# Stage ranks, delta-A weights on GpSimd and a last pair kept in SBUF, in a scan, attention and FFN kernel on one core

## The chip, the cores and the metric

The kernel runs on one core of a Trainium2 chip. The metric is the device time of one execution in microseconds. Engines are named as in the profile: PE (matmul), PEld (its weight loads), DVE (VectorE), ACT (ScalarE), POOL (GpSimd), and SP, whose queue issues all of this kernel's DMAs.

## What is computed

The input is x of shape (8, 96, 64, 64). Layer 0 is a selective-scan block with a residual, layer 1 an attention without softmax and a feed-forward with values rounded to 8-bit floats, each with a residual. Cut to what matters here:

```python
xh = layernorm(gn(x))                       # group norm, then layer norm over 96 channels
xi, z = split(xh @ in_proj.T)               # 192 channels each
xi = silu(depthwise_conv3x3(xi))            # 64 x 64 image
xs = [rows, columns, rows reversed, columns reversed](xi)      # K = 4 orders
dts, B, C = split(x_proj[k] @ xs[k])
delta = softplus(dt_proj[k] @ dts)
h = exp(delta * A) * h + (delta * u) * B;  y = sum(h * C)       # scan over 4096 steps
out = out_proj(layernorm(sum of 4 orders) * silu(z));  x = x + out
t = t + attention(ln(t));  t = t + ffn(ln(t))                   # per token of 96 channels
```

A is a weight, -exp(A_log). Eight images are worked on as four pairs.

## The kernel before

For each pair the function `vss_attn_ffn` runs three stages, and work of the pair before shares the first two:

1. **Project** (`project`, L369) with `back` (L825) of the previous pair. `project` normalises the two images in 16 blocks of 512 pixels and multiplies by the input weights; xi goes to padded tiles `ybuf` in SBUF and silu(z) to DRAM (`zs`). `back` adds the four scan orders in 16 blocks, transposes on PE (L880), normalises, projects out, adds the residual (`ta`, the new x) and normalises it for the attention (`tns`). It stores `ta` and `tns` to DRAM (`t1`, `tn`) and sums the attention's key-value products on PE (`pm`). When all 16 blocks are in, it makes one 97x96 matrix per image, `hm`.
2. **Convolve and prepare** (`convolve` L457, `prepare` L503) with `tail` (L963) of the previous pair. `convolve` does channel tiles 0 and 2 on DVE (L473 and L476: for each half of the image nine instructions of 2048 elements for each tile) and tile 1 on PE (nine matmuls with diagonal matrices per block of 512), then silu on ACT. `prepare` goes over two orders (rows, columns) of 8 chunks; in a chunk, for two directions and three tiles, it makes what the notes here call a unit: softplus on ACT (`d`), du = d*u on DVE (L560), and d split in three bf16 parts (ACT, DVE `rest` L571, ACT, POOL `dp` L576), stored to DRAM as `du` and `dl`. That is 96 units. The column order first copies xi transposed to `u` on POOL (L535). `tail` loads `t1` and `tn` again in 16 blocks and does the attention's matmul with `hm`, a norm and the feed-forward.
3. **Scan** (`scan`): 1024 scan instructions on DVE (L743) for each pair, with 512 products on POOL (L707).

After the fourth pair's scan, `back` of that pair runs alone, and then `tail` of it alone.

**What sets the order.** Stages 1 and 2 record their operations in a `Plan`, with an engine, a cost, what they read and write, the ring of buffers that they take, and a rank. `Plan.run` then writes the program: again and again it takes the operation that can start first by these costs, and among those of an engine that could start within 0.1 us of its earliest, the one of lowest rank. An engine executes its instructions in the order written. The ranks in stage 2 are -2 for the convolution's first half of the image and -1 for its second (`-2 + h`), -1 + c/10 for the silus of chunk c, 0 to 1 for prepare's chunks ((o * NCH + c) / 16), and i/16 for the tail's blocks. Rings hold back blocks: `P.ring("chunk", [None] * 3)` lets three blocks of project be under way, and the PSUM banks of 2 KB are named rings, `q=3, hold=2`. In `norm` (L355) a `hold` bank is taken by the first matmul (L357) and given back by the last multiply (L365); between lie a square, a matmul (L361), ln and exp.

**The weights of delta * A** are made once, between stages 1 and 2 of the first pair, by `decay_weights` (L282), outside any `Plan`. DVE negates exp(A_log), splits it in three bf16 parts (L291 to L296), which are stored to DRAM (`ad`) and read back in another layout (`ac`, L311); for each of four directions DVE multiplies 128 x 6144 elements by a mask (L317) and SP stores the product (`awd`, L322). The product's operands are a broadcast of `ac` along its third axis and of the mask along its second and fourth:

```python
nc.vector.tensor_tensor(aw,                                   # [128, 48, 16, 8] bf16
    ac.rearrange("p (c n) -> p c n", n=8).unsqueeze(2).to_broadcast([128, 48, 16, 8]),
    mask.unsqueeze(1).unsqueeze(3).to_broadcast([128, 48, 16, 8]), ALU.mult)
```

The pool of these tiles is closed before `xi`'s is opened (`xp`, after `decay_weights()`).

Of the kernel before, what the change touches and what calls it, by code (L numbers as in the profile page):

```python
# [10 lines left out]
F32 = mybir.dt.float32  # L11
# [145 lines left out]
def vss_attn_ffn(ctx: ExitStack, tc: tile.TileContext, a: dict):  # L157
# [124 lines left out]
    def decay_weights():  # L282
# [4 lines left out]
        with tc.tile_pool(name="aprep", bufs=1) as wp:  # L287
            am = wp.tile([128, KD, 2, NS], F32, name="am")
            nc.sync.dma_start(am, a["alog"])
            nc.scalar.activation(am, am, AF.Exp)  # L290
            nc.vector.tensor_scalar(am, am, -1.0, None, ALU.mult)  # L291
            for i in range(3):
                ap = wp.tile([128, KD, 2, NS], BF16, name=f"ap{i}")
                nc.vector.tensor_copy(ap, am)
                if i < 2:
                    nc.vector.tensor_tensor(am, am, ap, ALU.subtract)  # L296
                for k in range(KD):
                    nc.sync.dma_start(ad[i, k, 0:128], ap[:, k, 0])
                    nc.sync.dma_start(ad[i, k, 128:DI], ap[0:64, k, 1])
# [8 lines left out]
            for k in range(KD):  # L308
                ac = wp.tile([128, NE * NS], BF16, name="ac", bufs=2)
                for i, rows, n in ((0, slice(0, 96, 2), 6), (1, slice(1, 96, 2), 6), (2, slice(96, 128), 4)):  # L310
                    nc.sync.dma_start(  # L311
                        ac[rows],
                        ad[i, k].rearrange("(s c) n -> s (c n)", s=8).unsqueeze(0)
                        .to_broadcast([n, 8, NE * NS]),
                    )
                aw = wp.tile([128, 48, 16, 8], BF16, name="awp", bufs=2)
                nc.vector.tensor_tensor(  # L317
                    aw,
                    ac.rearrange("p (c n) -> p c n", n=8).unsqueeze(2).to_broadcast([128, 48, 16, 8]),
                    mask.unsqueeze(1).unsqueeze(3).to_broadcast([128, 48, 16, 8]), ALU.mult,  # L320
                )
                nc.sync.dma_start(awd[k], aw.rearrange("p c m n -> p (c m n)"))  # L322
# [45 lines left out]

    def project(P, pair, zs, ybuf, p1):  # L369

# [10 lines left out]
        ring(P, p1, "zt", 2, [128, 2, F])  # L381
        P.ring("chunk", [None] * 3)
        stat = [[p1.tile([DIM, w], F32, name=f"{n}{b}") for n, w in (
# [73 lines left out]
    def convolve(P, xi, ybuf, p1):  # L457
# [3 lines left out]
        for t in range(9):  # L461
            dve(P, 0.28, lambda t=t: nc.vector.tensor_scalar(
                diag[:, t, :], ident, convw[:, 0, t : t + 1], None, ALU.mult), (), (f"diag#{t}",), (), -2)
        for h in range(2):
            for T in (0, 2):
                for t in range(9):
# [5 lines left out]
                    if t == 0:  # L472
                        dve(P, 1.4, lambda o=o, v=v, w=w: nc.vector.tensor_scalar(  # L473
                            o, v, w, None, ALU.mult), (), wr, (), -2 + h)
                    else:
                        dve(P, 2.34, lambda o=o, v=v, w=w: nc.vector.scalar_tensor_tensor(  # L476
                            o, v, w, o, ALU.mult, ALU.add), (), wr, (), -2 + h)
            for c in range(4 * h, 4 * h + 4):
                r0 = c * ROWS
                n = f"pc.{c}"  # L480
                for t in range(9):
                    dy, dx = divmod(t, 3)
                    mm(P, 0.87, lambda n=n, t=t, r0=r0, dy=dy, dx=dx: nc.tensor.matmul(  # L483
                        P[n], diag[:, t, :], pad[1][:, r0 + dy : r0 + dy + ROWS, dx : dx + HH],
                        start=(t == 0), stop=(t == 8)), (f"diag#{t}",), (n,), ((n, "big"),), -2 + h)
                act(P, lambda c=c: xi[1][:, bass.ts(c, F)], lambda n=n: P[n], AF.Identity, 0.68, (n,),
                    (f"xi1#{c}",), (), -2 + h, bias=convb[:, 0:1])
        for c in range(NCH):
            for T in range(3):
                b_ = 0.0 if T == 1 else convb[:, half(T) : half(T) + 1]  # L490
                act(P, lambda T=T, c=c: xi[T][:, bass.ts(c, F)], lambda T=T, c=c: xi[T][:, bass.ts(c, F)],
                    AF.Silu, 0.72, (), (f"xi{T}#{c}",), (), -1 + c / 10, "silu", bias=b_)

# [330 lines left out]

    def back(P, pair, ys, us, zs, t1, tn, tmp, psm):  # L825
        tns = ring(P, tmp, "tns", 3, [DIM + 1, F])
        for i, t in enumerate(tns):
            nc.gpsimd.memset(t[DIM : DIM + 1], 1.0)
        ring(P, tmp, "yk", 2, [128, KD, 8, 4 * NE])
# [5 lines left out]
        ring(P, tmp, "g", 2, [DIM, 2, F])  # L835
        ring(P, tmp, "ta", 2, [DIM, F])
        ring(P, tmp, "kv", 2, [128, 2, 2, DIM])
# [3 lines left out]
        for i in range(2 * NCH):  # L841
# [120 lines left out]

    def tail(P, pair, t1, tn, tmp):  # L963
        tfs = ring(P, tmp, "tf", 3, [DIM + 1, F])
        for t in tfs:
            nc.gpsimd.memset(t[DIM : DIM + 1], 1.0)
        ring(P, tmp, "xa", 3, [DIM, F])
        ring(P, tmp, "t2", 4, [DIM, F])
# [4 lines left out]
        ring(P, tmp, "ot", 2, [DIM, F])  # L973
        P.ring("unit", [None] * 3)
        for i in range(2 * NCH):
            c, b = divmod(i, 2)
            cs = bass.ts(c, F)
            rank = i / 16
            n = f"t.{i}"
            tf, xa, pa, t2, tq, hq, p2, y16, ot = (  # L980
                v + n for v in ("tf", "xa", "pa", "t2", "tq", "hq", "p2", "y16", "ot"))
            dma(P, 0.2, lambda tf=tf: P[tf][0:DIM], lambda b=b, cs=cs: tn[b, :, cs], (), (tf,), ((tf, "tf"),), rank)
            dma(P, 0.2, lambda xa=xa: P[xa], lambda b=b, cs=cs: t1[b, :, cs], (), (xa,), ((xa, "xa"),), rank)
            P.unit = f"unit.{n}"
            mm(P, 0.9, lambda pa=pa, b=b, tf=tf: nc.tensor.matmul(  # L985
                P[pa][:DIM], hm[b], P[tf], start=True, stop=True), (tf,), (pa,), ((pa, "q"),), rank)
            dve(P, 0.69, lambda t2=t2, xa=xa, pa=pa: nc.vector.tensor_tensor(
# [36 lines left out]
    for pair in range(npair + 1):  # L1024
# [11 lines left out]
        with ExitStack() as pads, ExitStack() as xis:  # L1036
# [4 lines left out]
            with ExitStack() as st:  # L1041
                st.enter_context(tc.manual_schedule())
                P = Plan()
                tmp = st.enter_context(tc.tile_pool(name="bk", bufs=1))
                psum = banks(P, st, q=3, hold=2, **({"py": 2} if old else {}))
                ring(P, tmp, "small", 6 if old else 8, [DIM, F])
                if old:
                    back(P, pair - 1, old["ys"], old["us"], old["zs"], old["t1"], old["tn"], tmp, psum)
                if new:
                    project(P, pair, new["zs"], ybuf,  # L1050
                            st.enter_context(tc.tile_pool(name="p1", bufs=1, side="right")))
                P.run(table)
# [5 lines left out]
            with ExitStack() as st:  # L1058
# [128 lines left out]
```

## Time and profile before

| what | us |
|---|---|
| median of 3 runs | 10556.45 |
| lowest and highest | 10539.96 and 10565.98 |
| the profiled execution, and its span | 10552.56 and 10550.8 |
| first scan instruction of pairs 0 to 3, from the span's start | 638.9, 3228.7, 5821.8, 8417.2 |
| end of the last scan instruction of pairs 0 to 3 | 2414.6, 5005.4, 7598.9, 10192.6 |
| first instruction of the convolution on DVE, pairs 0 to 3 | 230.5, 2729.4, 5320.1, 7914.2 |
| last dp on POOL, pairs 0 to 3 | 614.6, 3204.3, 5796.7, 8390.8 |
| last pair: hm made; last block of the tail; end of the span | 10437.7; 10547.3; 10550.8 |

Times in the profile run from the span's start. A group's line gives line, engine, operation, the tiles written and read, and a count; behind the bar come busy time, the mean of one in ns, and the idle time before them with who ended it. In a table by stretch each engine has its busy us and its count of instructions. The clock column is the share of TensorE's clock that was granted, the DMA column the mean busy share of the 16 DMA engines.

### The profile page before, as it was taken

Reading aid. Unit: us, or ns where it says so; the run is one execution under the profiler, and the core shown is the slowest. Engines: PE = TensorE matmul, PEld = TensorE weight load, DVE = VectorE, ACT = ScalarE, POOL = GpSimd, SP = SyncE. Lnnn points to the kernel's source line nnn. Section 1 sums busy time; section 2 is a strip of 40 time slices with the busy share of each in tenths; the row PEclk is TensorE's granted clock in tenths of the full one; section 3 lists DMA queues with packets and bytes.
Section 4 is the critical chain, followed back from the end, with each engine's and each line's share of the span. In section 5 each row is a group of like instructions: output and inputs, shape, how many; then the busy total and the mean of one; then the engine's idle time right before and its main releaser. Section 6 shows DMA issues by size and latency. Waiting matters only on the chain. (4 is left out here: it accounts for less than half of the span.)

```text
span 10550.8 us, 377529 instructions
## 1 busy us (share of the span) xinstructions
PE 7647.5 (72%) x163328; PEld 5376.1 (51%) x163328; DVE 9068.0 (86%) x6702; ACT 6962.8 (66%) x12201; POOL 7996.9 (76%) x2802
## 2 busy tenths in 40 slices
PE   6766666668985676666987666776698666666678
PEld 2235555555324565555532555665553255555554
DVE  3689999996668999999566999999857699999985
ACT  3567777775566777776656677777665577777754
POOL 0579999992148999999124999999812599999961
PEclk8679999999878989999987889889897799989999
DMA  2787888879478888787947888888775778787885
GB/s 75 203 212 212 217 214 214 217 212 203 123 192 213 214 214 216 211 218 192 210 131 194 213 214 215 214 214 215 195 181 159 192 213 216 213 215 215 214 200 138
DMA packets 1597751, 2095.56 MB, mean 199 GB/s; under 512 B 407603, under 2 KB 1048116, under 8 KB 1592500
## 3 DMA queue, kind: packets, MB, share of 16 engines
q1 hardware_dynamic: 1596084, 2071.39, 75.6%
q8 instruction: 1283, 21.02, 0.9%
q14 instruction: 384, 3.15, 0.1%
HBM read 1606.82 MB, written 464.01 MB: 196 GB/s over the span
## 5 line engine op out<-in xcount | busy, mean ns | idle before, releaser
L743 DVE TENSOR_TENSOR_SCAN h<-da,dbu 128x774 f32<-128x774 f32 x4096 | 7026.7, 1759 | 128.2 <-POOL dbu L707 43.4
L707 POOL TENSOR_TENSOR dbu<-dut,bc 128x1536 f32<-128x1536 f32 x2048 | 7083.5, 3601 | 60.8 <-DMA dm<-dl 42.4
L732 ACT ACTIVATE da<-da 128x768 f32<-128x768 f32 x4092 | 3260.2, 797 | 1985.0 <-PE da L725 1970.1
L725 PE MATMUL da<-dm,aw 128*128 128x128 bf16 x24576 | 2282.4, 235 | 2329.8 <-DVE h L743 2089.6
L725 PEld LDWEIGHTS <-aw 128*128 128x128 bf16 x24576 | 1793.6, 104 | 2574.9 <-issue 2287.7
L761 PE MATMUL yp<-h,cw 128*32 128x48 f32 x131072 | 2902.4, 238 | 78.7 <-issue 65.7
L761 PEld LDWEIGHTS yp<-h,cw 128*32 128x32 f32 x131072 | 2410.2, 154 | 527.2 <-issue 207.0
L661 ACT ACTIVATE cw<-bc,blk 128x512 f32<-128x512 f32 x2048 | 1472.6, 720 | 81.5 <-DMA dm<-dl 81.5
L576 POOL TENSOR_TENSOR dp<-rest,dp 128x512 bf16<-128x512 f32 x384 | 456.8, 1194 | 665.3 <-ACT dp L332 620.0
L866 POOL TENSOR_TENSOR yd<-yk 128x768 f32<-128x768 f32 x64 | 125.6, 1962 | 779.6 <-DMA yk<-ys 407.1
L535 POOL COPY u<-xi 128x512 f32<-128x512 f32 x96 | 205.3, 2153 | 534.4 <-ACT xi L332 502.1
L555 PE MATMUL big<-S,dtw 12*128 12x512 f32 x768 | 521.1, 805 | 120.2 <-ACT d L332 96.0
L769 ACT ACTIVATE yev<-yp 128x384 f32<-128x384 f32 x1024 | 505.6, 494 | 64.5 <-PE yp L761 64.2
L571 DVE TENSOR_TENSOR rest<-d,dp 128x512 f32<-128x512 f32 x384 | 345.0, 904 | 207.6 <-ACT dp L332 161.2
L332 ACT ACTIVATE dp<-rest 128x512 bf16<-128x512 f32 x384 | 239.2, 628 | 304.6 <-DVE rest L571 303.5
L704 ACT COPY dbu<-h 128x12 f32<-128x12 f32 x1984 | 409.3, 206 | 0.0
L555 PEld LDWEIGHTS big<-S,dtw 12*128 12x128 f32 x768 | 157.7, 231 | 439.0 <-ACT d L332 225.7
L332 ACT ACTIVATE small<-hold 96x512 f32<-96x512 f32 x192 | 113.8, 593 | 313.5 <-PE hold L357 295.8
L560 DVE TENSOR_TENSOR du<-d,u 128x512 f32<-128x512 f32 x192 | 210.1, 1102 | 118.9 <-ACT d L332 118.9
L880 PEld LDWEIGHTS py<-ident,yd 128*96 128x96 f32 x2048 | 245.4, 165 | 91.2 <-issue 83.9
L476 DVE SCALAR_TENSOR_TENSOR xi<-y,c_convw,xi 128x2048 f32<-128x2048 f32 x128 | 290.3, 2347 | 0.0
L483 PE MATMUL big<-y,diag 128*128 128x512 f32 x576 | 260.2, 615 | 18.3 <-ACT xi L332 12.5
(122 smaller groups left out, 6009.5 us busy)
## 6 DMA issues: line engine op xcount, KB each, us to landing
dut<-du SPq DMA_DIRECT2D x2048, 384.0 KB
dm<-dl SPq DMA_DIRECT2D x1024, 288.0 KB
dl<-dp SPq DMA_DIRECT2D x256, 384.0 KB
dm<-dl SPq DMA_DIRECT2D x1024, 96.0 KB
ys<-yev SPq DMA_DIRECT2D x1024, 96.0 KB
du<-du SPq DMA_DIRECT2D x256, 256.0 KB
bc<-cs SPq DMA_DIRECT2D x512, 128.0 KB
bc<-bs SPq DMA_DIRECT2D x512, 128.0 KB
```

Source lines behind the costliest of these rows:

```text
L332: "ACT", cost, lambda: nc.scalar.activation(dst(), src_(), func, **kw),
L555: mm(P, 1.0, lambda pq=pq, k=k, T=T, S=S: nc.tensor.matmul(P[pq], dtw[64:76, k, T], P[S][64:76], start=True, stop=True), (S, "dtw"), (pq,) ...
L571: dve(P, 0.88, lambda rest=rest, d=d, dp=dp, w=w: nc.vector.tensor_tensor(w(rest), w(d), P[dp][:, :, 0], ALU.subtract), (d, dp + "#0"), (r ...
L576: P.add("POOL", 1.24, lambda rest=rest, dp=dp, w=w: nc.gpsimd.tensor_tensor(P[dp][:, :, 2], w(rest), P[dp][:, :, 1], ALU.subtract), (rest, ...
L661: nc.scalar.activation(cw[i % 2][:, :, :, m, :].rearrange("p z j t -> p (z j) t"), bc[i][:, 1].rearrange("p z (j t) -> p (z j) t", j=NB), ...
L704: nc.scalar.copy(start, segs(hs[s - 1][:, :, r])[:, :, :, 1 if back else TC])
L707: nc.gpsimd.tensor_tensor(segs(t)[:, :, :, 1:], dut[g].unsqueeze(1) .to_broadcast([128, 2, NI, TC]), bc[s // NB][:, 0, :, bass.ts(c % NB, ...
L725: nc.tensor.matmul(e[:, i], aw[k, r][:, i, z, :], dm[s // 2][:, NI * r + i, bass.ts(c % 2, TC)], start=True, stop=True,)
L732: nc.scalar.activation(e, e, AF.Exp)
L743: nc.vector.tensor_tensor_scan(hs[s][:, w, r][:, d], da[p % 3][:, o : o + W6][:, d], dbu[4 * s + r][:, w][:, d], 0.0, ALU.mult, ALU.add,)
L761: nc.tensor.matmul(y[32 * q : 32 * q + 32, 2 * NE * i : 2 * NE * i + 2 * NE] .rearrange("p (j r i) -> p i j r", j=2, r=NR), w[:, z, :, t], ...
L769: nc.scalar.activation(yev[s][:, :, o : o + 8, :].rearrange("p j i e -> p i j e"), y[:, 0 : 16 * NE].rearrange("p (i j e) -> p i j e", j=2 ...
```

## The change

1. **Ranks of stage 2.** The convolution's second half gets rank 0.2 instead of -1, and so do the silus of chunks 4 to 7; the first half keeps -2. The tail's blocks get 0.25 + 0.75 i/16 instead of i/16.
2. **Rings of stage 1.** In the first pair, where nothing shares the stage, project may have five blocks under way instead of three, with 4 `q` and 4 `hold` banks and 10 `small` tiles instead of 3, 2 and 8. In the other pairs these counts stay.
3. **Delta-A weights.** The six small operations and the four products of `decay_weights` go from DVE to GpSimd.
4. **The last pair.** `back` keeps `ta` and `tns` of all 16 blocks in four SBUF tiles of 4096 columns (`kept`), does not store them, and `tail` follows in the same plan with rank from 1.0. Its first matmul now names `hm` among what it reads, and its ring of blocks has a name of its own, `turn`. So this tail has the stage's banks, q=3 and hold=2, and 6 `small` tiles; before it had q=3, hold=1 and 4.

```diff
-            nc.vector.tensor_scalar(am, am, -1.0, None, ALU.mult)
+            nc.gpsimd.tensor_scalar(am, am, -1.0, None, ALU.mult)
             for i in range(3):
                 ap = wp.tile([128, KD, 2, NS], BF16, name=f"ap{i}")
-                nc.vector.tensor_copy(ap, am)
+                nc.gpsimd.tensor_copy(ap, am)
                 if i < 2:
-                    nc.vector.tensor_tensor(am, am, ap, ALU.subtract)
+                    nc.gpsimd.tensor_tensor(am, am, ap, ALU.subtract)
...
                 aw = wp.tile([128, 48, 16, 8], BF16, name="awp", bufs=2)
-                nc.vector.tensor_tensor(
+                nc.gpsimd.tensor_tensor(
...
-        P.ring("chunk", [None] * 3)
+        P.ring("chunk", [None] * (3 if beside else 5))
...
         for h in range(2):
+            first = 0.2 if h else -2
...
-                            o, v, w, None, ALU.mult), (), wr, (), -2 + h)
+                            o, v, w, None, ALU.mult), (), wr, (), first)
...
-                            o, v, w, o, ALU.mult, ALU.add), (), wr, (), -2 + h)
+                            o, v, w, o, ALU.mult, ALU.add), (), wr, (), first)
...
-                        start=(t == 0), stop=(t == 8)), (f"diag#{t}",), (n,), ((n, "big"),), -2 + h)
+                        start=(t == 0), stop=(t == 8)), (f"diag#{t}",), (n,), ((n, "big"),), first)
...
-                    AF.Silu, 0.72, (), (f"xi{T}#{c}",), (), -1 + c / 10, "silu", bias=b_)
+                    AF.Silu, 0.72, (), (f"xi{T}#{c}",), (), -1 + c / 10 if c < 4 else 0.2, "silu", bias=b_)
...
-    def back(P, pair, ys, us, zs, t1, tn, tmp, psm):
-        tns = ring(P, tmp, "tns", 3, [DIM + 1, F])
-        for i, t in enumerate(tns):
-            nc.gpsimd.memset(t[DIM : DIM + 1], 1.0)
+    def back(P, pair, ys, us, zs, t1, tn, tmp, psm, kept=None):
+        if kept is None:
+            tns = ring(P, tmp, "tns", 3, [DIM + 1, F])
+            for t in tns:
+                nc.gpsimd.memset(t[DIM : DIM + 1], 1.0)
+            ring(P, tmp, "ta", 2, [DIM, F])
+        else:
+            for ring_, tiles in zip(("ta", "tns"), kept):
+                P.ring(ring_, [t[:, bass.ts(c, F)] for c in range(NCH) for t in tiles])
+            for t in kept[1]:
+                nc.gpsimd.memset(t[DIM : DIM + 1], 1.0)
...
-            dma(P, 0.2, lambda b=b, cs=cs: t1[b, :, cs], lambda ta=ta: P[ta], (ta,), (), (), rank + 0.2)
-            dma(P, 0.2, lambda b=b, cs=cs: tn[b, :, cs], lambda to=to: P[to][0:DIM], (to,), (), (), rank + 0.2)
+            if kept is None:
+                dma(P, 0.2, lambda b=b, cs=cs: t1[b, :, cs], lambda ta=ta: P[ta], (ta,), (), (), rank + 0.2)
+                dma(P, 0.2, lambda b=b, cs=cs: tn[b, :, cs], lambda to=to: P[to][0:DIM], (to,), (), (), rank + 0.2)
...
-    def tail(P, pair, t1, tn, tmp):
+    def tail(P, pair, t1, tn, tmp, after=None):
...
-            rank = i / 16
+            rank = (after or 0.25) + 0.75 * i / 16
...
+            if after is None:
...
+            else:
+                tf, xa = f"tnsb.{i}", f"tab.{i}"
+            P.unit = f"turn.{n}"
...
-                psum = banks(P, st, q=3, hold=2, **({"py": 2} if old else {}))
-                ring(P, tmp, "small", 6 if old else 8, [DIM, F])
+                psum = banks(P, st, **({"q": 3, "hold": 2, "py": 2} if old else {"q": 4, "hold": 4}))
+                ring(P, tmp, "small", 6 if old else 10, [DIM, F])
                 if old:
-                    back(P, pair - 1, old["ys"], old["us"], old["zs"], old["t1"], old["tn"], tmp, psum)
+                    kept = None
+                    if not new:
+                        kept = [[tmp.tile([DIM + i, L], F32, name=f"kept{i}{b}") for b in range(2)] for i in range(2)]
+                    back(P, pair - 1, old["ys"], old["us"], old["zs"], old["t1"], old["tn"], tmp, psum, kept)
+                    if kept:
+                        tail(P, pair - 1, old["t1"], old["tn"], tmp, 1.0)
...
-                if old:
+                if old and new:
                     ring(P, tmp, "small", 4, [DIM, F])
                     tail(P, pair - 1, old["t1"], old["tn"], tmp)
```

More of the change, by code (lines that the diff above doesn't have):

```diff
@@ L367, in norm, with project @@
             ("ncp" + n, "nrs" + n), written, new, rank)
-    def project(P, pair, zs, ybuf, p1):
+    def project(P, pair, zs, ybuf, p1, beside):
         pad = [t.rearrange("p (h w) -> p h w", w=HH + 2) for t in ybuf]
@@ L484, in convolve @@
                         P[n], diag[:, t, :], pad[1][:, r0 + dy : r0 + dy + ROWS, dx : dx + HH],
-                        start=(t == 0), stop=(t == 8)), (f"diag#{t}",), (n,), ((n, "big"),), -2 + h)
+                        start=(t == 0), stop=(t == 8)), (f"diag#{t}",), (n,), ((n, "big"),), first)
                 act(P, lambda c=c: xi[1][:, bass.ts(c, F)], lambda n=n: P[n], AF.Identity, 0.68, (n,),
-                    (f"xi1#{c}",), (), -2 + h, bias=convb[:, 0:1])
+                    (f"xi1#{c}",), (), first, bias=convb[:, 0:1])
         for c in range(NCH):
@@ L835, in back @@
         ring(P, tmp, "g", 2, [DIM, 2, F])
-        ring(P, tmp, "ta", 2, [DIM, F])
         ring(P, tmp, "kv", 2, [128, 2, 2, DIM])
@@ L961, in back @@
                 hm[b][DIM : DIM + 1], hm[b][DIM : DIM + 1], bff[DIM : DIM + 1], ALU.add), (), (f"hm{b}",), (), 1)
-    def tail(P, pair, t1, tn, tmp):
[L964 to L967, printed above, removed]
+    def tail(P, pair, t1, tn, tmp, after=None):
+        if after is None:
+            tfs = ring(P, tmp, "tf", 3, [DIM + 1, F])
+            for t in tfs:
+                nc.gpsimd.memset(t[DIM : DIM + 1], 1.0)
+            ring(P, tmp, "xa", 3, [DIM, F])
         ring(P, tmp, "t2", 4, [DIM, F])
@@ L973, in tail @@
         ring(P, tmp, "ot", 2, [DIM, F])
-        P.ring("unit", [None] * 3)
+        P.ring("turn", [None] * 3)
         for i in range(2 * NCH):
@@ L981, in tail @@
                 v + n for v in ("tf", "xa", "pa", "t2", "tq", "hq", "p2", "y16", "ot"))
-            dma(P, 0.2, lambda tf=tf: P[tf][0:DIM], lambda b=b, cs=cs: tn[b, :, cs], (), (tf,), ((tf, "tf"),), rank)
-            dma(P, 0.2, lambda xa=xa: P[xa], lambda b=b, cs=cs: t1[b, :, cs], (), (xa,), ((xa, "xa"),), rank)
-            P.unit = f"unit.{n}"
+            if after is None:
+                dma(P, 0.2, lambda tf=tf: P[tf][0:DIM], lambda b=b, cs=cs: tn[b, :, cs], (), (tf,), ((tf, "tf"),), rank)
+                dma(P, 0.2, lambda xa=xa: P[xa], lambda b=b, cs=cs: t1[b, :, cs], (), (xa,), ((xa, "xa"),), rank)
+            else:
+                tf, xa = f"tnsb.{i}", f"tab.{i}"
+            P.unit = f"turn.{n}"
             mm(P, 0.9, lambda pa=pa, b=b, tf=tf: nc.tensor.matmul(
-                P[pa][:DIM], hm[b], P[tf], start=True, stop=True), (tf,), (pa,), ((pa, "q"),), rank)
+                P[pa][:DIM], hm[b], P[tf], start=True, stop=True), (tf, f"hm{b}"), (pa,), ((pa, "q"),), rank)
             dve(P, 0.69, lambda t2=t2, xa=xa, pa=pa: nc.vector.tensor_tensor(
@@ L1044, in vss_attn_ffn @@
                 tmp = st.enter_context(tc.tile_pool(name="bk", bufs=1))
-                psum = banks(P, st, q=3, hold=2, **({"py": 2} if old else {}))
-                ring(P, tmp, "small", 6 if old else 8, [DIM, F])
+                psum = banks(P, st, **({"q": 3, "hold": 2, "py": 2} if old else {"q": 4, "hold": 4}))
+                ring(P, tmp, "small", 6 if old else 10, [DIM, F])
                 if old:
-                    back(P, pair - 1, old["ys"], old["us"], old["zs"], old["t1"], old["tn"], tmp, psum)
+                    kept = None
[4 more added lines that the diff above has]
+                        tail(P, pair - 1, old["t1"], old["tn"], tmp, 1.0)
                 if new:
                     project(P, pair, new["zs"], ybuf,
-                            st.enter_context(tc.tile_pool(name="p1", bufs=1, side="right")))
+                            st.enter_context(tc.tile_pool(name="p1", bufs=1, side="right")), bool(old))
                 P.run(table)
```

## The prediction

> **What bounds it now.** I read the page first, then busy time by stretch, then the stage borders in the timelines. The page gives no engine the whole span:
>
> ```profile
> span 10550.8 us, 377529 instructions
> PE 7647.5 (72%) x163328; PEld 5376.1 (51%) x163328; DVE 9068.0 (86%) x6702; ACT 6962.8 (66%) x12201; POOL 7996.9 (76%) x2802
> L743 DVE TENSOR_TENSOR_SCAN h<-da,dbu 128x774 f32<-128x774 f32 x4096 | 7026.7, 1759 | 128.2 <-POOL dbu L707 43.4
> ```
>
> The scan line runs in four clusters (639 to 2415, 3229 to 5005, 5822 to 7599, 8417 to 10193 us), each bound by DVE. They are 7100 us and the change leaves them alone. What it can move is the 3450 us between them. Columns here are stretch, its length, then PE, PEld, DVE, ACT, POOL busy, TensorE clock, DMA share, GB/s:
>
> ```profile
> 53.00:186.00 133.00, 92.68 (x152) 31.46 (x150) 23.04 (x48) 86.54 (x124) 0.00 (x0) 0.78 0.15 42
> 186.00:230.00 44.00, 32.67 (x72) 14.17 (x72) 26.14 (x4) 0.12 (x1) 0.00 (x0) 0.89 0.46 171
> ...
> 308.00:639.00 331.00, 238.05 (x370) 66.26 (x371) 195.27 (x199) 189.48 (x329) 160.35 (x124) 0.67 0.86 222
> ...
> 2729.00:2807.00 78.00, 78.00 (x171) 32.78 (x170) 78.00 (x40) 22.05 (x34) 13.25 (x1) 0.94 0.23 75
> 2807.00:3205.00 398.00, 320.13 (x549) 98.59 (x547) 246.74 (x341) 264.70 (x448) 166.50 (x136) 0.71 0.74 193
> ```
>
> Row 1 is pair 0's project stage (nobody full: latency). Row 2 is the delta-A weights: DVE does 26 us, everybody waits. Row 3 is pair 0's prepare: DMA 0.86. Row 4 is pair 1's convolution: DVE full, DMA at 0.23. Row 5 is its prepare with the tail of pair 0. So the convolution has idle queues and prepare has busy ones: the two could overlap, if nothing else binds both.
>
> Something does. While DVE convolved in pair 0, one GpSimd copy lasted 35 us instead of 1.04 (min/median/max in ns):
>
> ```profile
> L535 POOL COPY u<-xi x6: 1042/1284/35305, 276.4 to 319.9; 128x512 f32<-128x512 f32 x6
> ```
>
> And the weights: who ended the waits of 186 to 232 us, and the products' durations.
>
> ```profile
> ACT xi L332 <- DMA awd<-awp: 44.6, 1, 44.6
> DVE awp L317 <- DMA ac<-ad: 20.3, 1, 20.3
> ...
> DVE xi L473 <- DMA awd<-awp: 5.2, 1, 5.2
> ```
> ```profile
> L317 DVE TENSOR_TENSOR awp<-ac,mask x4: 6554/6558/6559, 199.0 to 218.7; 128x6144 bf16<-128x6144 bf16 x4
> ```
>
> DVE's first convolution instruction does not start when DVE is free; it waits until the last product has been written out. The built program says why: the tiles xi0 and xi1 lie in the memory that the weights' pool gave back, over both awp buffers.
>
> **What the Trainium skill says.** SBUF — State Buffer, "Who interferes with whom": a VectorE instruction with two SBUF inputs and a GpSimd instruction that reads SBUF exclude each other, and whichever starts first keeps the port for its whole length. The trace agrees: the 35.3 us copy above; afterwards, at 1.04 us, the copies alternate with DVE's. GPSIMD Engine Reference, "3.1 Elementwise": two-input work takes about 2.6 cycles an element against VectorE's 1. The trace: 3565 ns for the 1536 elements of dbu, 1156 ns for the 512 of dp. ScalarE: Activation LUTs, "What ACT_TABLE_LOAD costs": 1283 ns and a drain of 1380 more. The trace has 1283 ns, and the next activation starts at once (113.52 + 1.28, then 114.81), so I price a switch at 1.28 us.
>
> **The change, part by part.** Sums are against the profiled execution, 10552.6 us (span 10550.8 and 1.8 around it), 3.9 under the median of three.
>
> *Project of pair 0* (hold 2 to 4, q 3 to 4, chunk 3 to 5, small 8 to 10). Before, ScalarE does two blocks a round; its loads of the ln table stand at 101.86 and 119.04, so a round is 17.2 us:
>
> ```profile
> 101.86 1.28 ACT L273 ACT_TABLE_LOAD   x1
> ...
> 107.76 0.59 ACT L332 ACTIVATE small<-hold 96x512 f32<-96x512 f32 x1 [2.31 <-PE hold L357]
> 109.47 0.69 ACT L332 ACTIVATE y<-q,inb 128x512 f32<-128x512 f32 x1 [1.11 <-PE q L432]
> 111.09 0.69 ACT L332 ACTIVATE y<-q,inb 64x512 f32<-64x512 f32 x1 [0.93 <-PE q L438]
> ```
>
> Two loads are 2.6 us, idle time is 44 us over eight rounds, 5.5 each, so 9.1 are work. The changed order has rounds of 2, 4, 4, 4 and 2 blocks. A round of four: 18.2 + 2.6 + 5.5 = 26.3 against 34.4. Three of them: **-24 us**. Floor: PE's 92.7 us over 16 blocks are 23.2 for four, so at best -33; if the idle time doubles too, -8.
>
> *Weights on GpSimd.* Row durations give (3565 - 1156)/1024 = 2.35 ns an element, 14.4 us for 6144. Four take 57.6 instead of 26.3: +31. In the new SP order two of the three row loads of the third product stand behind the second product's write, which waits for GpSimd: +4 for issue and landing. Six small operations (0.23 to 0.29 us on DVE): +1, their 24 stores still take 0.5 us each to issue. DVE gains nothing from being relieved: its first convolution instruction, and ScalarE's first xi, still wait for the last product (now GpSimd's) and its 5.2 us write. Behind the products on GpSimd stand only the dp subtractions, which need the convolution anyhow; behind the writes on SP the us, bs, du and dl stores, the same. Sum **+36 us**, all on the path. Bounds: the skill's 2.6 cycles at its 1.2 GHz make 13.3 us (+31); half as much again for rows of only 8 elements, which nothing here shows, 21.6 (+65).
>
> *Convolution ranks, pair 0.* In the new order DVE does half the convolution (38.7 us), five instructions of the second half, then the first chunks' du and rest with the other 13 between them. First-half silu, matmul and softplus took 13 us after that half (269.2 to 282.6), so first chunks start about 11 us after it instead of 39. But until chunk 3 is done, port time is 13 x 2.27 = 29.5 for convolution, 24 units of (0.605 + 0.605 + 1.156) = 57, and six u copies at 1.05: 92 us, some 100 with hand-overs. That is 111 from the half to unit 24; before it was 118.5 (269.2 to 387.7). **-7 us**; bounds -17 (port never idle) and +5 (six more table loads in the planned order, 1.28 each, and half the port's hand-overs exposed). The u copies no longer stand at the head of GpSimd's queue, where they blocked the first dp until 314.6; they stand in chunk 2, behind xi's last silu. Second-half us stores move behind du and dl on SP and are read only by back.
>
> *Pairs 1 to 3.* The same, with the tail's rank raised: its blocks now mix with chunks 4 to 7 and the second order; T10 to T15 still come in a bunch (before: T9 to T15, 42 us with DMA at 0.25). From the convolution's start to the last dp, DVE and GpSimd work is 78 (convolution) + 96 x 2.37 + 24 x 1.05 (u) + 16 x 4.4 (tail) = 400 of 475 us, DMA about 313 (0.23 of 78 and 0.74 of 398). There is idle time to win, but the order decides: mixed blocks cost 7.5 us each before (212 us for 48 units of 3 us and nine blocks), bunched ones 6. I take **-10 us** each, -30; bounds -30 and +8 each. The other stages of these pairs keep their order, instruction for instruction.
>
> *Last pair.* 32 stores and 32 loads of t1 and tn go, and the tail follows in the same plan with hold 2, small 6. Back is PE-bound at 12.84 us a block; late yk rows cost 2.2 us twice: -4. The load between back and tail was 2.85 us: -2. In the tail one hold bank spans c96, square, ln, exp and multiply, and a block takes 5.78 us:
>
> ```profile
> 10487.16 0.68 ACT L332 ACTIVATE small<-q,eps 96x512 f32<-96x512 f32 x1 [1.19 <-PE q L361]
> ...
> 10492.92 0.68 ACT L332 ACTIVATE small<-q,eps 96x512 f32<-96x512 f32 x1 [1.19 <-PE q L361]
> 10493.64 0.63 ACT L332 ACTIVATE small<-small 96x512 f32<-96x512 f32 x1
> ```
>
> PE is busy 4.2 of that. With two banks I take 4.7: 16 x 1.08 = -17. The ones-rows are 4096 long now, about 4 us each on GpSimd, before its first yd, which waits for DMA until 10210.6: hidden. Sum **-23 us**, bounds -33 and -8.
>
> Total -24 + 36 - 7 - 30 - 23 = -48: **10505 us**; own range 10480 to 10530.
>
> **Rivals.** *The overlap pays in full*: -15 in pair 0, -30 in each other pair, -25 at the end, 10435. For it: DMA at 0.23 during the convolution, and 75 us without port load. Against: two-input DVE work and GpSimd exclude each other. Chance 0.17.
> *The overlap pays nothing* (port, more table loads, bunches again): -24 + 36 - 23 = -11, 10542. For it: prepare's second order already runs on the port (480 to 500 us: DVE 12.9 and POOL 11.3 busy, so 24 of 20 us, each waiting for the other inside its rows). Chance 0.24.
> *Slower*: the product with its rows of 8 elements is far slower on GpSimd than long rows are. Place: between ad's landing and the first convolution. Net zero at 14.4 + 48/4 = 26.4 us each, 0.3% slower from 34.4; at 40 us 10607. For it: no GpSimd row here has such short runs. Against: dp's broken rows cost what long ones do. Chance 0.11.
> Forecast: 0.48.
>
> **Chances.** A measurement can tell 0.3%, 32 us, from no change. Forecast: 0.36 faster, 0.12 within. Full overlap: 0.17 faster. None: 0.05, 0.18, 0.01. Slow product: 0.02 within, 0.09 slower. Faster 0.58, within 0.32, slower 0.10. The range leaves out the slow product and half of full overlap: 10440 to 10560.
>
> **What would show it.** awp on POOL near 14.4 us and the first convolution 67 us after the ac rows (31.5 before); six table loads fewer in project (15 in that row-1 stretch before); first rest 11 to 15 us after the convolution's first half; tail's blocks at 4.7 us. Wrong if the convolution starts before the last awd write, or if prepare's DMA share stays above 0.85 while DVE convolves.

## The result, and the profile after

The changed kernel takes 10523.34 us (median of eight runs, 10511.02 to 10532.68) against 10556.5 before (10539.96 to 10567.89): ratio 0.9968, 95% interval 0.9957 to 0.9979, some 33 us faster. The forecast was 10505. The page's first lines and the scan's row:

```profile
span 10520.4 us, 377413 instructions
PE 7627.9 (73%) x163328; PEld 5364.6 (51%) x163328; DVE 9060.1 (86%) x6692; ACT 6981.1 (66%) x12219; POOL 8052.4 (77%) x2808
L744 DVE TENSOR_TENSOR_SCAN h<-da,dbu 128x774 f32<-128x774 f32 x4096 | 7027.3, 1759 | 131.3 <-ACT da L731 35.3
```

The scans are unchanged (7027.3 us busy). The shares say nothing of the rest; the stages do. Columns of the next view as in the prediction: project of pair 0, then the weights.

```profile
53.00:149.00 96.00, 78.64 (x151) 29.13 (x149) 21.89 (x44) 74.02 (x114) 2.25 (x6) 0.88 0.20 59
...
150.00:215.00 65.00, 32.85 (x72) 14.12 (x72) 0.00 (x0) 1.31 (x3) 42.00 (x4) 0.75 0.30 110
```

Project is 37 us shorter (96 where it was 133); ScalarE's idle time fell from 133 - 86.5 = 46.5 us to 22. In the 65 us of the second row DVE does nothing and ScalarE 1.3 us: GpSimd works for 42 us, the DMAs move the weights, and PE does its part of the convolution. The products, and who waited for them:

```profile
L317 POOL TENSOR_TENSOR awp<-ac,mask x4: 10518/10522/10527, 163.1 to 201.0; 128x6144 bf16<-128x6144 bf16 x4
...
  DVE xi L474: 77.4, 1
  ACT xi L332: 65.6, 1
```

A product takes 10.52 us, and both DVE's and ScalarE's first xi wait until the last one has been written out (`awd`): the convolution starts at 217.0.

Stages, in us, before and after (one profile each; the last column is the spread over the runs below that leave the stage as it was before):

| stage | before | after | other runs, unchanged |
|---|---|---|---|
| pair 0: span's start to last pad write | 184.8 | 147.6 | 184.4 to 185.9 |
| pair 0: last pad write to first convolution | 45.7 | 69.4 | 44.7 to 46.1 |
| pair 0: convolution's start to first scan | 408.4 | 396.7 | 407.8 to 409.4 |
| pairs 1 to 3: last scan to convolution, mean | 314.9 | 317.3 | 314.5 to 318.0 |
| pairs 1 to 3: convolution's start to first scan, mean | 501.3 | 497.6 | 499.1 to 503.0 |
| one scan stage, mean | 1776.2 | 1777.9 | 1775.1 to 1777.4 |
| last scan to hm | 245.1 | 252.2 | 243.3 to 247.9 |
| hm to last block of the tail | 109.7 | 95.0 | 109.9 to 110.5 |

Rows 4 and 6 have the same instructions in both kernels. The loss of row 4 lies within what one run differs from the next by, that of row 6 stands 0.5 us above it. I take both for that; no run shows a cause.

### The profile page after: what moved, and what is told of

Same layout as the page of the kernel before. It is cut to its first block, busy times and chain, and to the rows that moved or that the text cites. A ratio compares the mean times of both kernels' runs of the same rounds, so it can differ in the third digit from the quotient of the medians.

```text
span 10520.4 us, 377413 instructions
## 1 busy us (share of the span) xinstructions
PE 7627.9 (73%) x163328; PEld 5364.6 (51%) x163328; DVE 9060.1 (86%) x6692; ACT 6981.1 (66%) x12219; POOL 8052.4 (77%) x2808
## 3 DMA queue, kind: packets, MB, share of 16 engines
q8 instruction: 1283, 21.02, 0.9%
## 5 line engine op out<-in xcount | busy, mean ns | idle before, releaser
L744 DVE TENSOR_TENSOR_SCAN h<-da,dbu 128x774 f32<-128x774 f32 x4096 | 7027.3, 1759 | 131.3 <-ACT da L731 35.3
L762 PEld LDWEIGHTS yp<-h,cw 128*32 128x32 f32 x131072 | 2405.9, 153 | 540.7 <-issue 217.0
L577 POOL TENSOR_TENSOR dp<-rest,dp 128x512 bf16<-128x512 f32 x384 | 525.1, 1371 | 894.7 <-ACT dp L332 871.6
L556 PEld LDWEIGHTS big<-S,dtw 12*128 12x128 f32 x768 | 150.7, 223 | 429.3 <-ACT d L332 208.0
L477 DVE SCALAR_TENSOR_TENSOR xi<-y,c_convw,xi 128x2048 f32<-128x2048 f32 x128 | 315.3, 2509 | 0.0
L561 DVE TENSOR_TENSOR du<-d,u 128x512 f32<-128x512 f32 x192 | 204.6, 1078 | 97.1 <-ACT d L332 92.7
L1024 POOL TENSOR_TENSOR ot<-t,y 96x512 f32<-96x512 f32 x64 | 86.7, 1357 | 257.5 <-DVE y L1022 225.1
```

The source lines that it names most:

```text
L556: mm(P, 1.0, lambda pq=pq, k=k, T=T, S=S: nc.tensor.matmul(P[pq], dtw[64:76, k, T], P[S][64:76], start=True, stop=True), (S, "dtw"), (pq,) ...
L577: P.add("POOL", 1.24, lambda rest=rest, dp=dp, w=w: nc.gpsimd.tensor_tensor(P[dp][:, :, 2], w(rest), P[dp][:, :, 1], ALU.subtract), (rest, ...
L744: nc.vector.tensor_tensor_scan(hs[s][:, w, r][:, d], da[p % 3][:, o : o + W6][:, d], dbu[4 * s + r][:, w][:, d], 0.0, ALU.mult, ALU.add,)
L762: nc.tensor.matmul(y[32 * q : 32 * q + 32, 2 * NE * i : 2 * NE * i + 2 * NE] .rearrange("p (j r i) -> p i j r", j=2, r=NR), w[:, z, :, t], ...
```

## The experiments

Ratios are to the kernel before, measured on the same chip together with each run; its median was 10548.6 to 10554.1.

### The four parts, each alone on the kernel before

**Weights alone.**

```diff
-            nc.vector.tensor_scalar(am, am, -1.0, None, ALU.mult)
+            nc.gpsimd.tensor_scalar(am, am, -1.0, None, ALU.mult)
...
-                nc.vector.tensor_tensor(
+                nc.gpsimd.tensor_tensor(
                     aw,
```

> The kernel before, with only the delta-A weights moved to GpSimd (the edit of the change, no other part). Theory: all of it lies on the path, because the first convolution instruction waits for the last awd write: four products of 10.52 us instead of 6.56 are +16, the third product's row loads queue on SP behind the second write, which waits for GpSimd, +6.5: ac rows to first convolution 53.9 us instead of 31.5, the kernel +22 us (ratio 1.002). Rival A: DVE, freed of the products, makes up for it in the convolution: 0 us or less. Rival B: the fixed cost of the loads was only in the changed kernel's order: +16 us.

10576.26 us, ratio 1.0021 (1.0013 to 1.003): +22. The first convolution instruction is at 253.3 instead of 230.5. The theory holds with its size; DVE gains nothing from being relieved (408.4 and 407.8 us from convolution to scan).

**Rings alone.**

```diff
-        P.ring("chunk", [None] * 3)
+        P.ring("chunk", [None] * (3 if beside else 5))
...
-                psum = banks(P, st, q=3, hold=2, **({"py": 2} if old else {}))
-                ring(P, tmp, "small", 6 if old else 8, [DIM, F])
+                psum = banks(P, st, **({"q": 3, "hold": 2, "py": 2} if old else {"q": 4, "hold": 4}))
+                ring(P, tmp, "small", 6 if old else 10, [DIM, F])
```

> The kernel before, with only the wider rings of pair 0's project stage (hold 4, q 4, chunk 5, small 10). Theory: six table loads fewer and blocks in rounds of four: last pad write at 148 us instead of 185, and nothing after it gives that back: the kernel -37 us (ratio 0.9965). Rival: the weights' stage, which needs only alog and ScalarE's exponential, was hidden less in the shorter stage and gives some back: -24 us. Pairs 1 to 3 and the scans have the same instructions: each of their stages within 1 us of the kernel before, if the +14 us that they show in the changed kernel belong to another part or to the run.

10514.97 us, ratio 0.9964 (0.9952 to 0.9976): -38. Last pad write at 150.7, first scan at 605.0 instead of 638.9: nothing is given back. This part alone gives as much as the whole change. Which of the four rings it needs was not tried.

**Ranks alone.**

```diff
+            first = 0.2 if h else -2        # convolve: in place of -2 + h
...
-                    AF.Silu, 0.72, (), (f"xi{T}#{c}",), (), -1 + c / 10, "silu", bias=b_)
+                    AF.Silu, 0.72, (), (f"xi{T}#{c}",), (), -1 + c / 10 if c < 4 else 0.2, "silu", bias=b_)
...
-            rank = i / 16                   # tail
+            rank = 0.25 + 0.75 * i / 16
```

> The kernel before, with only the ranks of the convolution's second half, of its silu and of the tail beside it (rank 0.25 + 0.75 i/16). Theory: pair 0 from the convolution's first half to the last dp 333 us instead of 345 (-12), pairs 1 to 3 -4 each from the convolution's start to the first scan, because the tail's blocks, now behind, cost 6.6 us each against 5.6: together -24 us (ratio 0.9977). Rival A: the +2.4 us of each pair's first stage and +1.5 of each scan in the changed kernel come from this part (other DMA traffic at the borders): then -10 us. Rival B: the overlap pays nothing by itself, and pair 0's gain came from its earlier start: 0.

10542.52 us, ratio 0.9991 (0.9982 to 0.9999): -9. In its profile pair 0 takes 399.6 us from convolution to scan (408.4 before), pairs 1 to 3 take 497.2 (501.3 before). Rival A's number fits better than mine. Of its reason, the scans show nothing (1776.9 us, 1776.2 before); the first stages of pairs 1 to 3 took 317.0 (314.9 before), and all kernels with the old ranks lie at 314.5 to 316.5 there, those with new ones at 315.7 to 318.0. So a loss of a us or two per pair by the ranks is possible, and not shown.

**Last pair alone.** The `kept` tiles and the tail in back's plan, as in the change; nothing else.

```diff
+                    if not new:
+                        kept = [[tmp.tile([DIM + i, L], F32, name=f"kept{i}{b}") for b in range(2)] for i in range(2)]
...
+                    if kept:
+                        tail(P, pair - 1, old["t1"], old["tn"], tmp, 1.0)
```

> The kernel before, with only the last pair's rows kept in SBUF and its tail planned with back. Theory: from mean of the gain in the tail (hm to last ot 95 us instead of 110, -15: two hold banks instead of one, and no load) and the loss in back (last scan to hm 252 instead of 245, +7: the kept tiles take the low addresses, so that yk lies over the scan's last dm and starts 5 us later): -8 us (ratio 0.9993). Rival A: back loses nothing in a kernel without the other parts (its +7 is the run's): -15 us. Rival B: the tail's gain is eaten: 0. All other stages within 1 us of the kernel before.

10547.61 us, ratio 0.9995 (0.9989 to 1.0002): -5, not told apart from none by this measurement. In the profile the tail gains 11.3 (98.4 for 109.7) and back loses (248.5 for 245.1; 248.1 to 253.1 in all runs with kept rows, 243.3 to 247.9 in those without). By the ratios the four parts sum to +22 - 38 - 9 - 5 = -30, and the change gave -33: they are nearly independent.

### Where the overlap's gain went in pairs 1 to 3

**Old rank of the tail, on the changed kernel.**

```diff
-            rank = (after or 0.25) + 0.75 * i / 16
+            rank = (after or 0) + (0.75 if after else 1) * i / 16
```

> The changed kernel, with one edit: the tail's rank in pairs 1 to 3 is i/16 again, as before; the convolution's new ranks stay. Theory (the overlap's gain of pairs 1 to 3 is given back by the tail's blocks, put behind the first chunks, at 6.6 us each against 5.6): the stage from the convolution's start to the first scan takes 5 us less per pair than the 497.6 of the changed kernel, -15 us in all (10508, ratio 0.9954). Rival A (the raised rank is what lets the chunks start before the convolution ends, and without it the first rest comes after the whole convolution): +3.5 per pair, +10 us (0.9977). Rival B: the stage is bound by the sum of its DVE and GpSimd work on the shared port, in whatever order: 0.

10436.97 us, ratio 0.9896 (0.9882 to 0.9909): 86 us under the changed kernel in medians (76 by the ratios), more than five times what I expected, in the direction that I expected. Convolution to scan is 470 us for each of the three pairs. The two kernels' busy times, from the convolution's start to its end and from there to the last dp of pair 1. The changed kernel:

```profile
2709.50:2833.60 124.10, 110.95 (x213) 39.52 (x213) 116.02 (x75) 62.39 (x96) 39.60 (x19) 0.84 0.54 148
2833.60:3180.90 347.30, 286.98 (x507) 90.54 (x505) 212.19 (x304) 232.10 (x392) 146.67 (x117) 0.72 0.70 185
```

With the old rank:

```profile
2714.80:2860.20 145.40, 135.10 (x275) 49.62 (x275) 130.90 (x117) 81.93 (x132) 62.52 (x24) 0.85 0.54 150
2860.20:3160.20 300.00, 246.09 (x444) 76.52 (x442) 189.52 (x263) 204.62 (x350) 136.28 (x112) 0.76 0.77 202
```

With the old rank four tail blocks end beside the convolution, with the raised rank none. That makes the convolution 21 us longer and what follows 47 shorter. The engines' work is nearly the same (DVE 328.2 and 320.4, ScalarE 294.5 and 286.6): the difference is idle time. ScalarE's table loads in the same stretch, by line; the changed kernel first, then the old rank:

```profile
L332 ACT ACT_TABLE_LOAD x17 | 21.8, 1283 | 0.3
L273 ACT ACT_TABLE_LOAD x7 | 9.0, 1283 | 0.1
```
```profile
L332 ACT ACT_TABLE_LOAD x10 | 12.8, 1283 | 0.2
L273 ACT ACT_TABLE_LOAD x8 | 10.3, 1283 | 0.1
```

24 loads against 18. The kernel before has 18 here too, so the 31 us per pair by which this run is shorter than it (470 for 501) are not loads: the convolution's new ranks give them. What is one load worth?

**More table loads.**

```diff
-            made = nc.scalar.preload_act_table_set(LOGEXP)
-            tc.stamp_issue_order_token(made.ins, "tables")
+            for name in ("softplus", "silu_and_others") * more[0] + (LOGEXP,):   # more[0] = 1 in stage 2 of pairs 1 to 3
+                made = nc.scalar.preload_act_table_set(name)
+                tc.stamp_issue_order_token(made.ins, "tables")
```

> The changed kernel, with one edit: ahead of each load of the ln table in the stages of tail, convolution and prepare of pairs 1 to 3, the softplus and the silu table are loaded too, which are 12 table loads more per pair, 36 in all, in an order that is otherwise the changed kernel's. It prices one ACT_TABLE_LOAD on these stages. Theory (ScalarE is in the chain of both kinds of blocks, so that a load costs its 1.28 us): +46 us (10569, ratio 1.001); then the 6 loads that the raised tail rank costs explain 8 of the 28 us per pair that the old rank gained. Rival A: ScalarE is busy 294 of 471 us there, and loads fall into its gaps: +0 to +10 us. Rival B: a load costs more than itself, because PSUM banks and rings stand full behind it: +90 us.

10569.62 us, ratio 1.0016 (1.0009 to 1.0022): +46 for 36 loads in medians (51 by the ratios), 1.3 to 1.4 each, which is about their own length of 1.283. A load there is wholly on the path, though ScalarE is idle more than a third of the time. So the six extra loads of the raised rank explain 8 of the 27 us per pair, if they cost what these cost, which stand directly ahead of another load.

**Tail still earlier.**

```diff
-            rank = (after or 0.25) + 0.75 * i / 16
+            rank = (after or 0) + 0.6 * i / 16
```

> The changed kernel, with one edit: the tail's rank in pairs 1 to 3 is 0.6 i/16, ahead of the chunks beside it (i/16 gave 10437, 0.25 + 0.75 i/16 is the changed kernel). Theory (a tail block beside the convolution and the first order costs 2 us, because all engines have gaps there, and some 6 beside the second order, where DVE and GpSimd fill the port): the five blocks that still ran late with i/16 come early too, 20 us less in their place, 10 more in the chunks behind: -10 per pair against i/16, 10407 (ratio 0.9865). Rival A: the gaps are full with i/16 already: 10437. Rival B: the tail delays the first chunks and so all that follows: +10 per pair, 10467.

10439.95 us, ratio 0.989 (0.9876 to 0.9903): the same as i/16, rival A. It has 23 loads, five more than i/16, in a stage of the same length (468 to 475 us), so the loads alone don't set the time. I put most of the other 19 us per pair down to gaps that the blocks fill, and that are full with i/16. That is read from the stretches and from this run, and not shown: no single edit isolates it.

**The port.**

```diff
-                        P.add("POOL", 1.24, lambda rest=rest, dp=dp, w=w: nc.gpsimd.tensor_tensor(
+                        dve(P, 0.88, lambda rest=rest, dp=dp, w=w: nc.vector.tensor_tensor(
                             P[dp][:, :, 2], w(rest), P[dp][:, :, 1], ALU.subtract), (rest, dp + "#1"),
```

> The changed kernel, with one edit: the last subtraction of dp, 96 a pair, on DVE instead of GpSimd (same operands and sizes). Theory (prepare is bound by the port that two-input DVE work and GpSimd share; its sum is 0.605 + 0.605 + 1.156 = 2.37 us a unit, and would be 1.81): up to 0.55 x 96 = 53 us less per pair; since hand-overs and the tail stay, I take 25 per pair, -100 us in all (10423, ratio 0.987). Rival A (latency of the chain or ScalarE binds it): 0. Rival B (DVE's own queue becomes the bound: 0.6 x 96 = 58 us more DVE work in a pair, and nothing comes off the path): up to +58 per pair, +60 to +200 us (1.006 to 1.02).

10427.19 us, ratio 0.9883 (0.987 to 0.9897): -96 against the changed kernel. The groups over pair 1's stage, in the changed kernel and then with the subtraction on DVE:

```profile
L577 POOL TENSOR_TENSOR dp<-rest,dp 128x512 bf16<-128x512 f32 x96 | 130.8, 1366 | 230.1 <-ACT dp L332 230.0
L572 DVE TENSOR_TENSOR rest<-d,dp 128x512 f32<-128x512 f32 x96 | 88.9, 929 | 40.0 <-ACT dp L332 32.9 <-POOL dp L577 6.3 <-issue 0.7
```
```profile
L572 DVE TENSOR_TENSOR rest<-d,dp 128x512 f32<-128x512 f32 x96 | 71.1, 746 | 18.4 <-ACT dp L332 17.9
L577 DVE TENSOR_TENSOR dp<-rest,dp 128x512 bf16<-128x512 f32 x96 | 69.5, 727 | 51.7 <-ACT dp L332 48.8
```

219.7 us on the two engines became 140.6, and DVE's rest got faster although DVE has more to do, now that GpSimd's subtractions are gone from the port that both share. DVE's busy time in the stage rose by only 7 us (328.2 to 335.1). Pair 0, which has no tail, gained 10 to 15 us (386.5 for 396.7 to 401.4 in the kernels with the same pair 0); pairs 1 to 3 gained 27 each, but their order changed too: 17 table loads instead of 24, worth 9, and pair 0's has 8 instead of 10. So the port's wait is seen in rest (929 to 746 ns), but how much of either gain is its own can't be said: the subtraction itself is shorter on DVE (0.73 us, on GpSimd 1.16 even where nothing disturbed it), and no run separates a freer port from a shorter chain.

**Three edits together.** The weights go ahead of project as in the section on them.

```diff
-            rank = (after or 0.25) + 0.75 * i / 16
+            rank = (after or 0) + (0.75 if after else 1) * i / 16
...
-                        P.add("POOL", 1.24, lambda rest=rest, dp=dp, w=w: nc.gpsimd.tensor_tensor(
+                        dve(P, 0.88, lambda rest=rest, dp=dp, w=w: nc.vector.tensor_tensor(
...
+                decay_weights(late)
```

> The changed kernel with the three edits that paid one by one: tail rank i/16 (10437 alone), last dp subtraction on DVE (10427 alone), weights ahead of project on GpSimd (10487 alone). Weights and pair 0 add up (-36 and -12 against the changed kernel). For pairs 1 to 3 the question is whether the -27 of each of the two other edits are the same 27. Theory: mostly, since the plan with dp on DVE had 17 table loads per pair in that stage, as the old rank has 18, against 24 in the changed kernel, so both edits removed the same loads; what the port gives by itself is what pair 0 showed, 12 to 15 per pair: 10523 - 36 - 12 - 82 - 40 = 10353 (ratio to before 0.981). Rival A (wholly the same gain): 10393. Rival B (independent: order in one, port in the other): 10309.

10412.07 us, ratio 0.9872 (0.9856 to 0.9889), the fastest kernel measured, and slower than all three cases. Pair 0 adds up as expected: first scan at 562.0, 52 us before the changed kernel. Pairs 1 to 3 don't: 480 to 485 us from convolution to scan, 20 table loads, where either edit alone gave 470 with 18 or 17. The planner writes another order when an operation changes its engine, and this one took longer; why was not tried. The sums say that the weights with only one of the two others would be at 10390 to 10400; that was not run.

### The weights

**In memory of their own, on the changed kernel.**

```diff
-        with tc.tile_pool(name="aprep", bufs=1) as wp:
+        wp = late.enter_context(tc.tile_pool(name="aprep", bufs=1))   # late closes after stage 2
```

> The changed kernel, with one edit: the pool of the delta-A weights stays open until pair 0's convolution and prepare are done, so that xi0 and xi1 lie in other memory than the awp buffers. Theory (the convolution waits for the last awd write only because its output overlies that memory): the first convolution instruction starts at 153 us instead of 217 in the profile; the four products, 42 us of GpSimd, then share the port with the convolution and delay it by 0 to 42 us, so the kernel is 22 to 64 us faster than the changed one; I take 40 (10483 us, ratio to before 0.993). Rival A: the wait is for something else: the convolution still starts near 217, 0 us. Rival B: the products starve behind back-to-back convolution instructions, the awd writes come late, and us, bs, du and dl stores queue on SP behind them: pair 0's first scan no earlier than 614 us, 0 us or slower.

10514.58 us, ratio 0.9965 (0.9952 to 0.9977), against 0.9968. The convolution starts at 159.9 instead of 217.0, so the wait was for the memory; and the 57 us are gone by the 25th dp (370.3 against 367.8). The products:

```profile
L318 POOL TENSOR_TENSOR awp<-ac,mask x4: 10520/10746/53246, 164.8 to 246.0; 128x6144 bf16<-128x6144 bf16 x4
L323 SPq DMA_DIRECT2D awd<-awp x4: 326/327/345, 218.1 to 256.5; - x4
```

The first one takes 53.2 us instead of 10.5: it ends 10.4 us after DVE's first wait since the convolution began (1.7 us, at 207.7). The last ends at 256.5, and only then comes the first dp on GpSimd (done at 257.6, 12 us earlier than in the changed kernel). That is rival B.

**Ahead of project.**

```diff
+            if pair == 0:
+                decay_weights(late)          # ahead of stage 1; its DMAs by nc.gpsimd.dma_start
...
-            if pair == 0:
-                decay_weights()
```

> The changed kernel, with one edit: the delta-A weights are made ahead of pair 0's project stage, in memory of their own, and their 46 DMAs are issued on GpSimd's queue instead of SP's. Theory (the weights cost their whole length because they stand between project and convolution; with the memory apart, what took the gain back in the kernel before this one was the port that products and convolution share, and neither is left): GpSimd does the products beside project, where DVE is busy 23 of 133 us, the first convolution instruction starts near 155 us instead of 217, and the first scan comes 60 us earlier, near 555: -58 us (10465, ratio to before 0.992). Rival A: GpSimd's own issuing of 46 DMAs and the locks that its products put on DVE stretch project by the same: -10 to -30. Rival B: prepare of pair 0 is bound from its end, by DMA or the port, and not from its start: 0, as with the weights apart.

10486.55 us, ratio 0.9935 (0.9922 to 0.9949): -37 against the changed kernel. The products take 10.52 us each again and end at 112.5, but project's last pad write comes at 170.6 instead of 147.2 to 150.7. DVE in that time (start, duration, then line and tiles):

```profile
64.22 0.15 DVE L404 COPY gm<-q 96x1 f32<-96x1 f32 x1 [9.05 <-PE q L402]
64.41 16.15 DVE L405 TENSOR_TENSOR gd<-mv,gm 96x1 f32<-96x1 f32 x1
80.59 0.22 DVE L407 SCALAR_TENSOR_TENSOR gv<-gd,mv 96x1 f32<-96x1 f32 x1
```

One subtraction of 96 x 1 elements, 0.155 us long otherwise, waited 16 us until two products were through; all of the second image waits for it. A step of the norm waits 3.5 us more behind the fourth product (4.06 us instead of 0.54). That is rival A in kind, though -37 is more than its -10 to -30, and by the lock and not by the issuing (0.55 to 0.63 us for each `awd` write, in GpSimd's own free time). The rest of the gain stays: first scan at 578.6.

### Back of the last pair

**Kept rows behind the rings.**

```diff
         ring(P, tmp, "kv", 2, [128, 2, 2, DIM])
+        if kept is not None:
+            kept += [[tmp.tile([DIM + i, L], F32, name=f"kept{i}{b}") for b in range(2)] for i in range(2)]
```

> The changed kernel, with one edit: the kept rows are allocated behind back's rings instead of ahead of them, so that yk lies at 36000 to 60576 instead of 101536 to 126112. Theory (yk lies over the scan's last dm and waits for the last scan): the first yk load issues 5.7 us after the last scan instead of 10.5, last scan to hm 247 us instead of 252: -5 us (10518, ratio 0.9963). Rival A: back's longer time is the run's, since kernels with an unchanged back show 243.3 to 247.9 us for it: 0. Rival B: other tiles of back then lie over the scan's last ones: 0 in the time with a first yk that is earlier.

10517.34 us, ratio 0.9971 (0.9961 to 0.9981): the same. Back still takes 252.4 us. The loads of yk in the kernel before, in the changed kernel, then here, whose last scans end at 10192.6, 10170.1 and 10167.4:

```profile
L351 SPq DMA_DIRECT2D yk<-ys x96: 376/633/4856, 10198.3 to 10380.2; - x96
```
```profile
L351 SPq DMA_DIRECT2D yk<-ys x96: 376/626/4814, 10180.6 to 10363.9; - x96
```
```profile
L351 SPq DMA_DIRECT2D yk<-ys x96: 376/626/4727, 10178.2 to 10360.7; - x96
```

The first comes 10.5 and 10.8 us after the last scan, and 5.5 to 5.7 in the kernels without kept rows: my theory of the address is wrong. In the trace the first load now stands on SP behind the scan's last ys stores, before, it stood ahead of two of them. What makes that order, and whether it is all of back's 5 us, stays open.

## Why the prediction was right, and where it was not

The time lies in the range and near the forecast (-48 forecast, -33 measured), but that is luck, since errors cancel: rings and weights came out 10 to 14 us better each, pairs 1 to 3 and the last pair together some 38 us worse.

- **Project, -24: measured -34 to -38, below my floor of -33.** ScalarE's loads of the ln table mark the rounds:

```profile
62.38 1.28 ACT L273 ACT_TABLE_LOAD   x1
...
87.36 1.28 ACT L273 ACT_TABLE_LOAD   x1
...
112.27 1.28 ACT L273 ACT_TABLE_LOAD   x1
...
134.31 1.28 ACT L273 ACT_TABLE_LOAD   x1
```

 Three rounds of four blocks took 25.0, 24.9 and 22.0 us, 71.9 together, where I had 3 x 26.3 = 78.9; the six rounds of two before took 103.5 (66.83 to 170.33). That makes -32, and -29 with the rings alone. The other 5 to 6 us lie at the two ends of the stage, to which my sum gave nothing: the first of these loads comes 4.4 us earlier. My floor left out the ends, too, and it was no floor: at a granted clock of 0.88 the matmuls that were busy 92.7 us at 0.78 were busy 78.6, and the last round is shorter than its 23.2. Six table loads fewer was right (15 to 9). The idle time of the sum, 44 us, is 46.5 by the stretch.
- **Weights, +36: measured +22, below my bound of +31.** The mechanism was right (all on the path, DVE gains nothing). The term "2.35 ns an element, 14.4 us" was mis-sized: 10.52 us, 1.71 ns. It was the slope between two other rows, 3.565 us and 1.156 us. The estimate from the 2.6 cycles an element of the Trainium skill (GPSIMD Engine Reference, "3.1 Elementwise"), 13.3 us, was also too high. The waits for row loads were 6.5 us (190.5 - 184.1), where I took 4.
- **Ranks of pair 0, -7: measured -9** (408.5 in four kernels with the old ranks, 396.7 to 401.4 with the new). Right, and the first rest came 9.7 us after the convolution's first half, where I said 11.
- **Pairs 1 to 3, -10 each: measured -3.** I raised the tail's rank with the convolution's in one sum and asked only what the blocks cost where they go. The step left out is what they are worth where they would else have gone: with the old rank, four of them end beside the convolution, and fill gaps there as I read it (in the kernel before none ended there, since all of the convolution went first). With the ranks of the convolution alone the gain is 501 - 470 = 31 per pair. That is the case that I held at 0.17, "the overlap pays in full", with its number for these pairs; the second part of the same edit took it back, 8 of the 27 us by table loads.
- **Last pair, -23: measured -5 (the ratio of that part alone) to -8 (by its stages).** Tail with load -19: measured -11 to -15: the blocks still go in turns of three, 16.2 us a turn or 5.4 a block, for my 4.7. The two hold banks work as thought:

```profile
10440.98 0.59 ACT L332 ACTIVATE small<-hold 96x512 f32<-96x512 f32 x1 [0.66 <-PE hold L357]
10441.84 0.59 ACT L332 ACTIVATE small<-hold 96x512 f32<-96x512 f32 x1 [0.27 <-PE hold L357]
10442.76 0.68 ACT L332 ACTIVATE small<-q,eps 96x512 f32<-96x512 f32 x1 [0.33 <-PE q L361]
...
10457.14 0.59 ACT L332 ACTIVATE small<-hold 96x512 f32<-96x512 f32 x1 [0.67 <-PE hold L357]
```

 Back -4: measured +5 (means of the kernels with kept rows, 250.5, and without, 245.9). I counted the stores that go, and gave nothing to a first yk load that comes 5 us later; its cause stays open. The memsets were hidden as said (3.5 us each).
- **The slower rival** (products far slower in rows of 8) fell: 10.52 us.

## What to carry to other kernels

When an edit moves work later, price the place where it would else have stood as well as the place that it goes to: here the tail's four blocks were worth more beside the convolution than behind it. Where a planner writes the order, test each rank alone, and test a combination before adding up its parts: two edits that gave 27 us per pair each gave less together than either. Before making a wait shorter by moving memory, ask what the freed engines will then contend for.

## What the runs showed of the hardware

- A GpSimd product of a bf16 and an f32 input, both broadcast, with inner rows of 8 elements and a bf16 result took 10.52 us for 6144 elements a partition, 1.71 ns each, less per element than dbu's f32 rows (3565 ns for 1536, 2.32 ns).
- The port that the Trainium skill describes (SBUF — State Buffer, "Who interferes with whom") was not handed over between back-to-back instructions: a 0.155 us subtraction on DVE waited 16.15 us behind two GpSimd products, and a 10.5 us product on GpSimd took 53.2 us against convolution instructions. Two of DVE's `xt` multiplications with one input in PSUM ran beside the products (from 107.54 us, with the weights ahead of project) and took what the others take (670 to 687 ns). A DVE instruction with one tensor input, in SBUF, did wait once, 4055 ns for 539:

```profile
L429 DVE TENSOR_SCALAR xt<-xt,c_nw,c_nb x16: 525/539/4055, 52.1 to 162.1; 96x512 f32<-96x512 f32 x16
```

- An ACT_TABLE_LOAD cost 1.3 to 1.4 us of the kernel's time each (46 to 51 us for 36), about its own 1283 ns. Of the drain of 1380 ns that the Trainium skill adds (ScalarE: Activation LUTs, "What ACT_TABLE_LOAD costs"), these runs show nothing; the added loads stood directly ahead of another load.
